# Which row groups first: the issue order of in_proj and gates ahead of ssm_out in a scan kernel

## The chip, the cores and the metric

The kernel runs on one core of a Trainium2 chip. The metric is the device time of one execution in microseconds (us).

## The reference, cut to what matters

Input x is (4, 128, 96, 96) in fp32. It is group-normalised, laid out as four sequences (rows and columns, each forwards and backwards), and each sequence goes through the same chain:

```python
t = _grouped1x1(x, in_proj_w, in_proj_b, G)          # 128 -> 512 channels, 4 groups of 32
u, gate = (t[:, :HID], t[:, HID:])                   # HID = 256
u = jax.nn.silu(u)
u = lax.conv_general_dilated(u, dw_w, ...)           # depthwise, 5 taps
s = _conv1x1(u, ssm_in_w)                            # 256 -> 32 channels
...                                                  # a, bb, cc from u; prefix sums: hst
u = u + _conv1x1(cc * hst + ssm_d[None, :, None] * s, ssm_out_w)   # 32 -> 256: "ssm_out"
u = _grouped1x1(u * jax.nn.sigmoid(gate), mix_w, mix_b, G)
return _conv1x1(u, out_proj_w, out_proj_b)
```

The four results are fused by one more 1x1 convolution and added to x.

## The kernel before

The work is cut into 384 units of 384 positions. A unit has `s` = 0 or 1 (two of the four sequences run side by side); unit numbers alternate between the two, so I call the units with `s` = 0 even and those with `s` = 1 odd. The program is software-pipelined by hand: step `t` does in_proj for a unit 8 ahead, and gates, ssm_out and gating for the unit 12 behind. TensorE's order in a step is set by this code, not by a scheduler:

```python
def unit(t):
    ...
    rows(t + UB ..., bi ..., bk)           # pf (in_proj), pg (gates), pz (ssm_out)
    ...
    accumulate(units[bi - 1], bk)          # py: mix, out_proj and fuse in one matrix
    gating(units[bi])
    conv(un, 0, bk); ...                   # pc
    proj(t - 1, 0)  or  proj(t - 2, 1)     # pp
```

The change is in `rows`, which issues 16 matmuls of 32x32 (in_proj and gates; each on its own of the 16 tiles of 32x32: in the trace of before their first records start within 0.11 us and take 0.51 us each, so all 16 run side by side) and then 8 more of 32x32 (ssm_out):

```python
def mm(o, col, lhsT, rhs, start, stop):
    r = slice(32 * col, 32 * col + 32)
    nc.tensor.matmul(o[r, : rhs.shape[-1]], lhsT, rhs, start=start, stop=stop, ...)

def rows(i, bi, bk):
    ...
    for c in range(4):                     # column group c of the array
        if front:
            for j in range(2):             # pf: row groups 0 and 1
                r = slice(32 * j, 32 * j + 32)
                m, q = (c, g) if by_taps(s, j) else (g, c)
                mm(pf[j], c, wn[r, 32 * m : 32 * m + 32], x_in[s][r, q, :], True, True)
        if gate:
            q, off = gate_at(bu)
            for j in range(2):             # pg: row groups 2 and 3
                r = slice(64 + 32 * j, 96 + 32 * j)
                mm(pg[j], c, gwn[r, 32 * c : 32 * c + 32],
                   x_in[bu["s"]][r, q, off : off + N], True, True)
    if gate:
        pz = ps.tile([P, 2, 512], F32, tag="z", ...)
        for c in range(4):
            for j in range(2):             # pz: row groups s and 2 + s
                r = slice(64 * j + 32 * bu["s"], 64 * j + 32 * bu["s"] + 32)
                mm(pz[:, j, :], c, w_so[r, ...], z[r, bu["p"], :], True, True)
        gv = wk.tile([P, 2, N], F32, tag="gv", ...)
        for j in range(2):                 # ScalarE: gate, reads pg[0], then pg[1]
            nc.scalar.activation(gv[:, j, :], pg[j][:, :N], AF.Tanh, ...)
        nc.vector.tensor_add(pz[:, :, :N], pz[:, :, :N], bu["u"])
```

Ssm_out thus uses row groups 0 and 2 in even units, 1 and 3 in odd ones.

## Time and profile before

| before | value |
|---|---|
| time, 3 runs | 2598.93 us median (2598.4 to 2602.78) |
| TensorE busy | 2548.0 us, 98% of the profiled execution |
| VectorE, ScalarE busy | 2025.2 us (78%), 1572.9 us (60%) |
| matmul records | 40016, two for each fp32 matmul |
| DMA | mean 52 GB/s |

A busy share near 100% on one engine says where to look, not that the engine computes all the time: the ends of matmuls in the profile are modelled, and TensorE counts as busy all through the stage below, in which tiles stand idle (pz 2's for some 180 ns, as an estimate: free near 683, used at 865). So the single records of a stage have to be read. Below, "the stage" is pf, pg and pz of one step, its zero is the first pf record, and its end is the start of py. Times in the stage are in ns and are medians over the stages of which all records are there (181 even and 182 odd ones).

### The profile page before, as it was taken

To read this page: it belongs to the slowest core of one execution; us is meant where nothing else is said; L and a number is where in the kernel's file an instruction comes from. 1 tells how busy PE (TensorE), PEld (TensorE's weight loads), DVE (VectorE), ACT (ScalarE), POOL (GpSimd) and SP (SyncE) were. 2 spreads that over 40 slices of the span, in tenths; PEclk is the share of its full clock that TensorE was granted. 3 is DMA by queue.
4 is the path that set the end of the run, shared out by engine and by line. 5 is a ranking of instruction groups with operands and counts; after the bars stand their busy time and mean duration, and the time that the engine had idled before them with its cause. 6 is when DMAs were issued, how large, how long until landed. Compare 5 with 4: busy or idle time off the path is not lost.

```text
span 2605.0 us, 89269 instructions
## 1 busy us (share of the span) xinstructions
PE 2548.0 (98%) x40016; PEld 966.1 (37%) x40016; DVE 2025.2 (78%) x2727; ACT 1572.9 (60%) x2912; POOL 506.4 (19%) x786
## 2 busy tenths in 40 slices
PE   6999999999999999999999999999999999999997
PEld 3333333333333333333333333333333333333331
DVE  3688878877878887777887887778876788778876
ACT  4666666666656666666665666666665666666652
POOL 4211121111111112111111112111111111111110
PEclk8999999999999999999999999999999999999998
DMA  5112111112331211111241111111132111111011
GB/s 141 46 45 51 47 34 30 35 29 85 94 97 45 51 41 28 35 30 36 84 134 54 50 45 37 30 36 29 45 117 76 36 30 36 33 32 36 23 41 56
DMA packets 79278, 134.18 MB, mean 52 GB/s; under 512 B 11440, under 2 KB 73392, under 8 KB 78896
## 3 DMA queue, kind: packets, MB, share of 16 engines
q1 hardware_dynamic: 76704, 127.64, 17.8%
q8 instruction: 315, 5.16, 0.8%
q10 hardware_dynamic: 2192, 0.83, 0.1%
q14 instruction: 67, 0.55, 0.1%
HBM read 109.55 MB, written 18.87 MB: 49 GB/s over the span
## 4 chain that ended last, share of the span: by engine, by line
PE 95%; DVE 1%; DMA 1%; ACT 1%; issue 0%; SPq 0%; DVEq 0%; ACTq 0%
PE pc L317 28%; PE py L317 21%; PE pp L317 20%; PE pz L317 12%; PE pf L317 11%; PE pg L317 2%; DMA out<-acc 1%; DVE t L480 0%; DVE gv L323 0%; ACT t L446 0%; ACT gv L373 0%; DMA acc<-in_xr 0%; DMA x_in<-in_xs 0%; ACT L446 0%; ACT L182 0%
## 5 line engine op out<-in xcount | busy, mean ns | idle before, releaser
L317 PE MATMUL pc<-sil,band 128*32 128x384 f32 x9216 | 820.4, 488 | 0.5 <-ACT gv L373 0.4
L403 ACT COPY u<-pc 128x384 f32<-128x384 f32 x576 | 275.8, 479 | 554.2 <-PE pc L317 553.0
L317 PE MATMUL pp<-u,w_proj 128*32 128x384 f32 x6144 | 594.7, 488 | 7.1 <-ACT std L182 5.6
L317 PE MATMUL py<-gv,w_fin 128*32 128x384 f32 x6144 | 586.8, 500 | 7.9 <-ACT gv L373 5.8
L418 DVE SCALAR_TENSOR_TENSOR pt<-sil,w_tap,pt 128x384 f32<-128x384 f32 x576 | 358.5, 622 | 180.5 <-ACT pt L416 164.5
L373 ACT ACTIVATE gv<-pg,bnorm 128x384 f32<-128x384 f32 x768 | 402.8, 576 | 106.6 <-PE pg L317 106.6
L317 PEld LDWEIGHTS pc<-sil,band 128*32 128x32 f32 x9216 | 297.0, 110 | 458.3 <-issue 363.8
L317 PE MATMUL pz<-t,w_so 32*32 32x384 f32 x6144 | 432.2, 494 | 6.6 <-DVE gv L323 6.4
L460 DVE TENSOR_TENSOR t<-pp,t 64x384 f32<-64x384 f32 x192 | 173.2, 902 | 287.2 <-ACT t L452 287.1
L377 DVE TENSOR_TENSOR pz<-pz,u 128x768 f32<-128x768 f32 x384 | 369.8, 963 | 16.5 <-PE pz L317 10.6
L317 PE MATMUL pf<-x_in,wn 32*32 32x385 f32 x6144 | 360.3, 504 | 10.4 <-DVE acc L505 9.4
L323 DVE SCALAR_TENSOR_TENSOR gv<-gv,pz 128x768 f32<-128x768 f32 x384 | 362.7, 944 | 0.1
L317 PE MATMUL pg<-x_in,wn 32*32 32x384 f32 x6144 | 360.3, 496 | 0.0
L449 POOL TENSOR_SCALAR t<-t 64x384 f32<-64x384 f32 x192 | 181.6, 946 | 879.2 <-ACT t L446 879.2
L317 PEld LDWEIGHTS pp<-u,w_proj 128*32 128x32 f32 x6144 | 224.6, 109 | 303.0 <-issue 258.1
L488 POOL COPY t<-t 64x384 f32<-64x384 f32 x192 | 95.9, 500 | 1154.5 <-DVE t L487 1154.5
L381 ACT ACTIVATE sil<-pf,bsilu 128x385 f32<-128x385 f32 x576 | 313.9, 585 | 4.3 <-PE pf L317 4.1
L317 PEld LDWEIGHTS py<-gv,w_fin 128*32 128x32 f32 x6144 | 161.9, 110 | 406.2 <-issue 275.2
L452 ACT ACTIVATE t<-pp,b_proj 64x384 f32<-64x384 f32 x192 | 110.6, 576 | 243.0 <-PE pp L317 122.6
L446 ACT ACTIVATE t<-pp,b_proj 128x384 f32<-128x384 f32 x192 | 208.6, 1086 | 70.6 <-PE pp L317 53.9
L317 PEld LDWEIGHTS pz<-t,w_so 32*32 32x32 f32 x6144 | 167.7, 103 | 166.3 <-issue 92.7
L450 POOL TENSOR_SCALAR t<-t 64x384 f32<-64x384 f32 x192 | 182.6, 951 | 15.9
(65 smaller groups left out, 1468.6 us busy)
## 6 DMA issues: line engine op xcount, KB each, us to landing
x_in<-in_xs SPq DMA_DIRECT2D x96, 385.0 KB, 4.3
x_in<-in_xs SPq DMA_DIRECT2D x384, 96.2 KB, 2.4
out<-acc SPq DMA_DIRECT2D x24, 768.0 KB, 5.1
xs<-in_xr SPq DMA_DIRECT2D x72, 192.0 KB, 2.3
acc<-in_xr SPq DMA_DIRECT2D x18, 768.0 KB, 4.6
acc<-in_xr SPq DMA_DIRECT2D x24, 192.0 KB, 3.8
w_fuse<-in_fuse_wT ACTq DMA_DIRECT2D x1, 256.0 KB, 4.1
w_proj<-in_proj_wT ACTq DMA_DIRECT2D x1, 128.0 KB, 4.8
```

The costliest lines, as they stand in the source:

```text
L317: nc.tensor.matmul(o[r, : rhs.shape[-1]], lhsT, rhs, start=start, stop=stop, skip_group_check=True)
L323: nc.vector.scalar_tensor_tensor(gv, gv, 1.0, bu["pz"][:, :, :N], ALU.add, ALU.mult)
L373: nc.scalar.activation(gv[:, j, :], pg[j][:, :N], AF.Tanh, bias=gbn[:, 2 + j : 3 + j], scale=0.5)
L377: nc.vector.tensor_add(pz[:, :, :N], pz[:, :, :N], bu["u"])
L381: nc.scalar.activation(sil[:, j, g, :], pf[j][:, : N + 1], AF.Silu, bias=bn[:, j : j + 1] if by_taps(s, j) else bsil[:, j, g : g + 1],)
L403: nc.scalar.copy(un["u"][:, j, :], pc[:, :N])
L418: nc.vector.scalar_tensor_tensor(un["u"][:, j, :] if k == K - 1 else part, src, w_tap[:, k : k + 1], part, ALU.mult, ALU.add,)
L446: nc.scalar.activation(ta[:, p, :], pp[:, :N], AF.Tanh, bias=b_proj[:, 0:1])
L449: nc.gpsimd.tensor_scalar(a, a, half, DMIN + half, ALU.mult, ALU.add)
L450: nc.gpsimd.tensor_scalar(a, a, 0.9999, 0.0001, ALU.min, ALU.max)
L452: nc.scalar.activation(tb[0:64, p, :], pp[0:64, :N], AF.Tanh, bias=b_proj[0:64, 1:2])
L460: nc.vector.tensor_mul(ta[0:64, p, :], pp[64:P, :N], ta[0:64, p, :])
```

## The change

The intent: pz should find its tiles free sooner. The matmuls on the two row groups that this unit's ssm_out uses come first, in the order in which pz will use the tiles; then the other two row groups. Nothing is added or removed.

```diff
-        for c in range(4):
-            if front:
-                for j in range(2):
-                    r = slice(32 * j, 32 * j + 32)
-                    m, q = (c, g) if by_taps(s, j) else (g, c)
-                    mm(pf[j], c, wn[r, 32 * m : 32 * m + 32], x_in[s][r, q, :], True, True)
-            if gate:
-                q, off = gate_at(bu)
-                for j in range(2):
-                    r = slice(64 + 32 * j, 96 + 32 * j)
-                    mm(pg[j], c, gwn[r, 32 * c : 32 * c + 32],
-                       x_in[bu["s"]][r, q, off : off + N], True, True)
+        so = bu["s"] if gate else 0
+        for e in (so, 1 - so):
+            r, rg = slice(32 * e, 32 * e + 32), slice(64 + 32 * e, 96 + 32 * e)
+            for c in range(4):
+                if front:
+                    m, q = (c, g) if by_taps(s, e) else (g, c)
+                    mm(pf[e], c, wn[r, 32 * m : 32 * m + 32], x_in[s][r, q, :], True, True)
+                if gate:
+                    q, off = gate_at(bu)
+                    mm(pg[e], c, gwn[rg, 32 * c : 32 * c + 32],
+                       x_in[bu["s"]][rg, q, off : off + N], True, True)
```

## The prediction

> **What bounds the kernel now.** I read the page first: busy shares, the slices, then the chain that ended last.
>
> ```profile
> PE 2548.0 (98%) x40016; PEld 966.1 (37%) x40016; DVE 2025.2 (78%) x2727; ACT 1572.9 (60%) x2912; POOL 506.4 (19%) x786
> PE 95%; DVE 1%; DMA 1%; ACT 1%; issue 0%; SPq 0%; DVEq 0%; ACTq 0%
> PE pc L317 28%; PE py L317 21%; PE pp L317 20%; PE pz L317 12%; PE pf L317 11%; PE pg L317 2%; DMA out<-acc 1%; DVE t L480 0%; DVE gv L323 0%; ACT t L446 0%; ACT gv L373 0%; DMA acc<-in_xr 0%; DMA x_in<-in_xs 0%; ACT L446 0%; ACT L182 0%
> ```
>
> TensorE carries 95% of the chain; VectorE at 78% and ScalarE at 60% follow it. So the change can only pay through TensorE's own stream. It touches pf (in_proj), pg (gates) and, through what runs after them, pz (ssm_out). I therefore read one unit in the timeline of PE and of PEld (weight loads) in the middle of the run.
>
> ```profile
> 1203.70 0.51 PE L317 MATMUL pf<-x_in,wn 32*32 32x385 f32 x2
> 1203.71 0.51 PE L317 MATMUL pg<-x_in,wn 32*32 32x384 f32 x2
> ...
> 1203.79 0.52 PE L317 MATMUL pg<-x_in,wn 32*32 32x384 f32 x2
> 1204.04 0.49 PE L317 MATMUL pf<-x_in,wn 32*32 32x385 f32 x2
> ...
> 1204.37 1.12 PE L317 MATMUL pz<-t,w_so 32*32 32x384 f32 x16
> 1205.43 0.85 PE L317 MATMUL py<-gv,w_fin 128*32 128x384 f32 x8
> ```
>
> Each fp32 matmul leaves two records. The 16 matmuls of pf and pg fill the 16 tiles of 32x32: 16 first records start in 0.11 us, and the 16 second ones begin 0.35 us after the first of all. Then pz, 8 matmuls on 8 of these tiles, takes 1.06 us to the start of py. Two rounds like those before would be near 0.7 us. So there is something to win in pz; the question is what withholds it. The weight loads tell:
>
> ```profile
> 1204.05 0.10 PEld L317 LDWEIGHTS pz<-t,w_so 32*32 32x32 f32 x1
> 1204.37 0.10 PEld L317 LDWEIGHTS pz<-t,w_so 32*32 32x32 f32 x1 [0.22 <-issue]
> 1204.56 0.20 PEld L317 LDWEIGHTS pz<-t,w_so 32*32 32x32 f32 x12
> ```
>
> Only the first pz matmul starts early. The second has its weights loaded at 1204.56, 0.19 us later, although its tile came free near 1204.38. "Issue" says that no semaphore of another engine ended this gap.
>
> I then took the single records of the 361 rows stages whose records are all there, counted in ns from the first pf record. They differ by 1 ns or so, in two classes: even units (ssm_out on row groups 0 and 2) and odd ones (1 and 3).
>
> - second record of the first matmul: 347 in both
> - first pz record: 671 even, 678 odd; that is 324 after the second record of its own tile (347 and 354)
> - weight load of the second pz matmul: 861 in both
> - first records of pz 2 to 8: 865 to 965 in both, 16.7 apart; their second records: up to 1309 in both
> - start of py: 1734 even, 1720 odd
>
> [...] Before the stage, pp's last four matmul records start at -436 to -416 with a length of 486, and end at 50 to 70. [...] Observed: the 14th starts at 87, and in odd units the 15th and 16th at 102 and 118, 16 apart instead of 6.7. [...]
>
> [...] pz 1's weights load at 349, two ns after a matmul on its own row group began. [...] 15 later matmuls start before the second record of the first.
>
> [...] from the last pp record to the first pf record is 416 ns, where rounds of one mode follow at 323; so some 93 ns per change, twice a unit. The change leaves the number of mode changes alone.
>
> **The change part by part.** It removes and adds no instruction: still 16 matmuls of pf and pg, 8 of pz, the same waits, the same banks. The program order of the built kernels shows pf and pg of the unit's own row groups alternating over the four columns, then the other two; pz in its old order. Waits for the second pair of banks move from place 2 and 4 to 9 and 10; in before none of them held the stage, since 416 is the start in every class.
>
> 1. First pz matmul. Its tile is now the first issued in both classes, so it starts at 671 in odd units too: 7 ns earlier. But its second record (993 to 1000) has slack: the stage ends with pz 8's second record at 1309. Worth 0.
> 2. Pz 2 to 8. Their tiles were free well before use already: pz 2's near 683 against 865, and pz 8's near 770 to 786 against 965. Freeing them earlier (pz 8's tile would be the 8th, free at about 347 + 47 + 323 = 717) buys nothing[...] Worth 0.
> 3. A small term. In odd units the first matmul now lies on row group 1, not 0. Py starts 14 ns sooner after row groups 1 and 3 than after 0 and 2, at equal ends of pz, so I take a matmul one row group further on to be finished about 14 ns sooner. If that holds, pz 2 to 8 and the stage end come 14 ns sooner in odd units: 192 x 14 ns = 2.7 us. I count half: 1.3 us.
> 4. Other engines. ScalarE gets one pf and one pg bank some 60 ns earlier, the others at the same time; it isn't on the chain.
> 5. First 8 units (no gates) and last 20 (gates only): orders change inside 16 or 8 matmuls on free tiles; 0.
>
> Sum: 2598.9 - 1.3, so about 2597.5 us.
>
> **The rivals.** (a) The full gain that the edit aims for. If pz followed tile by tile as they came free, pz 8 would start near 770 and end its second record near 1093 + 323 instead of 1309 + 323: 216 ns x 384 units = 83 us, 3.2%, so 2516. For it: the tiles of pz do stand idle. Against: in before pz 2's tile stands idle for 180 ns in every unit, so the order of tiles isn't the wait. (b) [...] pz 2's load would wait for the last matmul on its row group. That one starts its second record at about 441 to 447 (even) or 463 (odd) and would at 347 + 47 = 394 after the change: 50 to 70 ns x 384 = 19 to 27 us, so about 2575. Against: 861 is the same in both classes though these starts differ by some 20 ns. (c) Slower: two row groups instead of four share the first 8 matmuls, and if loads or moving data of one row group got in each other's way the 6.7 ns steps would widen. [...] Against: pz itself uses this order of tiles, and in the last units[...] the timeline shows it at full pace:
>
> ```profile
> 2590.72 0.21 PEld L317 LDWEIGHTS pz<-t,w_so 32*32 32x32 f32 x16 [1.56 <-issue]
> 2590.75 0.88 PE L317 MATMUL pz<-t,w_so 32*32 32x384 f32 x16 [0.89 <-DVE gv L323]
> 2591.56 0.53 PE L317 MATMUL py<-gv,w_fin 128*32 128x384 f32 x4
> ```
>
> Here the same 8 matmuls reach py in 0.81 us, not 1.06, with first records 6.7 ns apart. [...]
>
> **Range and chances.** The three runs of before spread from 2598.4 to 2602.8. With (b) given one chance in ten and (a) one in twenty, I take 2597.5, 8 in 10 between 2588 and 2603; faster by over 2% 0.05, within 2% 0.92, slower 0.03.
>
> **What would show it.** Right: first pz record at 671 in odd units; second pz load still at 861 (847 in odd ones if point 3 holds); pz to py near 1.06 us; the chain at 95% PE with the same shares. Wrong: the pz loads follow each other from about 0.68 us on, or at about 0.80 (rival b), or the 16 first records take more than 0.11 us (rival c).

## More of the kernel before

One more part matters in the end: five PSUM banks go round between the steps, by this table.

```python
banks.append({"f": (w, x), "g": (y, z), "y": y, "c": (z, None), "t": h})   # even step
banks.append({"f": (w, x), "g": (z, y), "y": h, "c": (z, y), "t": None})   # odd step
```

## The result, and the profile after

The changed kernel took 2591.26 us (median of 4 runs, 2590.04 to 2596.08), the kernel before, in the same rounds, 2598.66 us (4 runs, 2596.43 to 2602.78). The ratio is 0.9973, with a 95% interval of 0.9955 to 0.9991: within 2%, though the interval leaves out 1. Here and below a ratio is the mean time of one kernel's runs over that of the other's of the same rounds, so it is not quite the ratio of the medians quoted.

This is inside the predicted range, but 6 us below the predicted time. The page of the changed kernel, its busy shares and its chain of waits:

```profile
PE 2534.8 (98%) x40016; PEld 964.0 (37%) x40016; DVE 2023.1 (78%) x2727; ACT 1554.8 (60%) x2912; POOL 512.2 (20%) x786
...
PE 95%; DVE 1%; ACT 1%; DMA 1%; issue 0%; DVEq 0%; ACTq 0%
PE pc L317 29%; PE py L317 21%; PE pp L317 20%; PE pz L317 12%; PE pf L317 11%; PE pg L317 2%; DVE gv L323 0%; DVE t L479 0%; DMA out<-acc 0%; ACT t L445 0%; DMA acc<-in_xr 0%; ACT gv L372 0%; DMA x_in<-in_xs 0%; ACT L445 0%; ACT L182 0%
```

Nothing has moved but small shares: `pz` still has 12% of the chain. One difference is easily overlooked: `DMA out<-acc` went from 1% to 0%. It comes back below.

The timeline of one even unit, TensorE, after (columns: start in us, length in us, engine, line, operation, output and inputs, how many):

```profile
1228.30 0.51 PE L317 MATMUL pf<-x_in,wn 32*32 32x385 f32 x1
1228.31 0.51 PE L317 MATMUL pg<-x_in,wn 32*32 32x384 f32 x1
...
1228.41 0.50 PE L317 MATMUL pg<-x_in,wn 32*32 32x384 f32 x1
1228.65 0.48 PE L317 MATMUL pf<-x_in,wn 32*32 32x385 f32 x1
...
1228.97 1.12 PE L317 MATMUL pz<-t,w_so 32*32 32x384 f32 x16
```

And its weight loads (in brackets the idle time before a load, and what ended it):

```profile
1228.65 0.10 PEld L317 LDWEIGHTS pz<-t,w_so 32*32 32x32 f32 x1
1228.97 0.10 PEld L317 LDWEIGHTS pz<-t,w_so 32*32 32x32 f32 x1 [0.22 <-issue]
1229.16 0.18 PEld L317 LDWEIGHTS pz<-t,w_so 32*32 32x32 f32 x10
1230.02 0.16 PEld L317 LDWEIGHTS py<-gv,w_fin 128*32 128x32 f32 x8 [0.62 <-ACT gv L372]
```

Pf and pg now alternate one by one, as the edit wants. The second pz matmul still gets its weights 0.86 us into the stage (1229.16 - 1228.30), as before: the edit's aim is missed. But py starts 1.05 us after the first pz record (1230.02 - 1228.97), where it was 1.06. Over all stages:

| ns from the stage's start | first pz record | load of pz 2 | tanh of pg[0] | start of py |
|---|---|---|---|---|
| before, even | 671 | 861 | 1100 to 1680 | 1734 |
| before, odd | 678 | 861 | 1100 to 1682 | 1720 |
| after, even | 671 | 860 | 983 to 1565 | **1720** |
| after, odd | 671 | 860 | 1117 to 1700 | 1720 |

(In a quarter of the odd stages the tanh starts only near 2367. Py starts at 1720 in these too.)

So it is the even units that gained 14 ns, not the odd ones, and the column that moved with them is ScalarE's. ScalarE in this even unit, before (the stage starts at 1203.70):

```profile
1204.80 0.58 ACT L373 ACTIVATE gv<-pg,bnorm 128x384 f32<-128x384 f32 x1
```

and after (the stage starts at 1228.30):

```profile
1229.28 0.58 ACT L372 ACTIVATE gv<-pg,bnorm 128x384 f32<-128x384 f32 x1
```

The tanh that reads pg[0] began 1.10 us into the stage and now begins 0.98 us into it. Now the table of banks tells the rest: in an even step py ("y": y) is written to the very bank that pg[0] ("g": (y, z)) has just held. So the program has py wait for that tanh (the view of waits below names it 189 times). Before, the tanh ended at 1680 and py started 54 later, at 1734. In an odd step py goes to bank h, which neither gate of that step holds, and py starts at 1720, which is 411 after the last pz record (1309), about the 416 from pp to pf at the other change of tile shape; within one shape (pp) the records of a tile follow at 323. After, the tanh of even units ends at 1565, 155 before 1720, and holds nothing.

The view of TensorE's waits had said so before the change (columns: us in total, times, longest in us):

```profile
PEld py L317 <- ACT gv L373: 128.7, 189, 2.5
```

and says almost the same after it:

```profile
PEld py L317 <- ACT gv L372: 124.5, 190, 2.5
```

There are 192 even units, and all 189 waits lie in even units: all of them but three. I had seen this line and put it down to the 411 ns after pz, which odd units have too. It was both: of a mean gap of 0.68 us (128.7 over 189) only the last 14 ns were ScalarE's own, the rest is the wait for pz. The new line shows why the name alone proves nothing: ScalarE is still named, though it is now done 155 ns ahead.

Fourteen ns in 192 units are 2.7 us (the expectations below say 2.6). The measured difference is larger. In all runs together, before has a mean of 2598.1 us (25 runs) and after one of 2590.2 (10 runs): 7.9 us. So a second cause of some 5 us is to be found. I cut both traces at the starts of py. Units 140 to 188, with nothing but the steady stage, took 309.93 us before and 309.60 after: 0.33 us over 24 even units, 13.7 ns for each, which is the 14 ns above and nothing more. Units 280 to 296 took 111.4 us before and 105.6 after. There the third batch of four ends: its last rows of `acc` go out, the next batch's rows are loaded into the same place, and VectorE's first addition to it has to wait. The waits there, before:

```profile
DVE acc L505 <- DMA x_in<-in_xs: 8.2, 1, 8.2
...
PEld pf L317 <- DVE acc L505: 5.5, 1, 5.5
```

and after:

```profile
DVE acc L504 <- DMA x_in<-in_xs: 4.9, 1, 4.9
...
PEld pf L317 <- DVE acc L504: 2.2, 1, 2.2
```

TensorE's next pf waits for VectorE, VectorE for a transfer, and both waits became 3.3 us shorter. The transfer named is a load of x_in, but the one that counts is the last load of `acc`: in both traces the addition begins 0.32 us after that load has landed (2007.98 and 2008.30 us before, 2003.06 and 2003.38 after), and in a later run, even_only, it begins 0.07 us before the named load of x_in lands. The loads of `acc` wait in turn for transfers that go out. The first of the two pairs, as SyncE issues it, before:

```profile
1989.65 0.35 SPq L515 DMA_DIRECT2D out<-acc  x1
1994.63 0.33 SPq L517 DMA_DIRECT2D acc<-in_xr  x1
```

and after:

```profile
1988.02 0.35 SPq L514 DMA_DIRECT2D out<-acc  x1
1991.57 0.33 SPq L516 DMA_DIRECT2D acc<-in_xr  x1
```

The load is issued 0.02 us after the outgoing transfer has landed, which took 4.97 us before and 3.53 after. (The page's median over all 24 outgoing transfers went from 5.1 to 3.6; here it is this one that is waited for.) There is one more difference: by the trace's record of the granted clock, TensorE ran at half speed for 6.8 us of units 280 to 296 before, and for none of them after. So the 5.8 us there are 3.3 of a shorter wait and, as an estimate, up to 3.4 (half of 6.8) of clock.

After this, the questions for the experiments were: is it the place in TensorE's stream that holds pz (rather than tiles or row groups)? Do the even units win through ScalarE? And do the other 5 us belong to the change, to one half of it, or to chance?

### The profile page after: what moved, and what is told of

Its sections match the earlier page's. It is cut to its first block, busy times and chain, and to the rows that moved or that the text cites. A ratio compares the mean times of both kernels' runs of the same rounds, so it can differ in the third digit from the quotient of the medians.

```text
span 2589.8 us, 89224 instructions
## 1 busy us (share of the span) xinstructions
PE 2534.8 (98%) x40016; PEld 964.0 (37%) x40016; DVE 2023.1 (78%) x2727; ACT 1554.8 (60%) x2912; POOL 512.2 (20%) x786
## 4 chain that ended last, share of the span: by engine, by line
PE 95%; DVE 1%; ACT 1%; DMA 1%; issue 0%; DVEq 0%; ACTq 0%
PE pc L317 29%; PE py L317 21%; PE pp L317 20%; PE pz L317 12%; PE pf L317 11%; PE pg L317 2%; DVE gv L323 0%; DVE t L479 0%; DMA out<-acc 0%; ACT t L445 0%; DMA acc<-in_xr 0%; ACT gv L372 0%; DMA x_in<-in_xs 0%; ACT L445 0%; ACT L182 0%
## 5 line engine op out<-in xcount | busy, mean ns | idle before, releaser
L317 PE MATMUL py<-gv,w_fin 128*32 128x384 f32 x6144 | 580.0, 495 | 6.2 <-ACT gv L372 4.2
L445 ACT ACTIVATE t<-pp,b_proj 128x384 f32<-128x384 f32 x192 | 187.0, 974 | 70.2 <-PE pp L317 53.8
```

The costliest lines, as they stand in the source:

```text
L445: nc.scalar.activation(ta[:, p, :], pp[:, :N], AF.Tanh, bias=b_proj[:, 0:1])
```

## The experiments

All kernels are edits of `rows`. They use two helpers that hold the bodies of the loops of the changed kernel, unaltered: `pf_mm(e, c)` and `pg_mm(e, c)` issue one matmul of in_proj or gates on row-group pair `e` and column `c`; `pz_all()` issues the 8 of ssm_out. Every result was correct.

### The kernels again

The unchanged pair first. `after_again` is the changed kernel, in 5 rounds.

> The changed kernel once more, beside the runs of the others. Steady state as in its first profile: py starts 1720 ns after the first pf record in even and odd units, the second pz load comes at 860. If the steady 14 ns in every second unit are all that the order gives, the time lies 2 to 3 us below before (0.999); if the whole 7 us of the first comparison belong to the order, 0.997.

Measured: 2588.57 us (6 runs, 2584.11 to 2595.68) against 2597.84 for before (11 runs, 2588.83 to 2603.26), ratio 0.9968 [0.995, 0.9986]. The gain is there again, and larger than the 2.7 us of the steady stage. Units 140 to 188 again took 309.60 us, and units 280 to 296 took 104.8.

`before_again` and `before_third` are the kernel before with no edit, one look each, to see what two traces of one program differ in.

> The kernel before once more, for its profile. The steady parts must repeat (py at 1734 and 1720). If what the changed kernel gains beyond the steady 2.6 us is chance (waits for transfers and half-clock windows at the changes of batch and at the end), then the stretches in which the first profile of before was slow differ here: units 30 to 50 (136.4 us there, 134.65 in the changed kernel), 280 to 296 (111.4 against 105), 362 to 382 (111.7 against 104.3). If they belong to the order, they repeat within 0.5 us.

> The same as before_again, a third profile of before: chance gives values that differ among the three profiles, the order gives the same three times.

Measured: 2602.8 and 2601.14 us, where the timed runs of before in that call had a median of 2595.19 (3 runs). The steady stretch is the same to 0.01 us (309.92 in both). Others are not: units 30 to 50 took 136.4, 134.75 and 136.4 us in the three traces of before, the last 20 units 111.7, 111.6 and 109.4, and units 280 to 296 took 111.4, 108.9 and 111.5. In after, the two traces have 134.65 and 134.67, 104.34 and 104.35, 105.6 and 104.8. Such steps of 1.7 us and more come and go in one and the same kernel. By the rule set down above that speaks for chance in all three stretches, so a difference in one counts only if several traces bear it out.

### Only one half of the units

`even_only` and `odd_only` use the new order in the units of one kind, the old one in the others (`so == 1` in place of `so == 0` for odd_only):

```diff
-        for e in (so, 1 - so):
-            for c in range(4):
-                pf_mm(e, c)
-                pg_mm(e, c)
+        if gate and so == 0:
+            for e in (so, 1 - so):
+                for c in range(4):
+                    pf_mm(e, c)
+                    pg_mm(e, c)
+        else:
+            for c in range(4):
+                for e in range(2):
+                    pf_mm(e, c)
+                for e in range(2):
+                    pg_mm(e, c)
```

> New order only in units whose ssm_out uses row groups 0 and 2 (even), old order in odd units and in the front-only start. Theory A (in even units py writes the bank that held pg0, so it waits for ScalarE's tanh of pg0; the new order finishes pg0 sooner[...]): py at 1720 in even and in odd units, the whole steady gain of 2.6 us is here, 2591 to 2597 us. Rival B (a matmul on a later row group is finished sooner, my point 3 of the prediction, gain in odd units): py stays at 1734 in even units, no gain.

> New order only in odd units. Theory A: py 1734 even, 1720 odd, as before the change; time equal to before within 0.1%. Rival B: second pz load near 847 in odd units and py near 1706 there, 2.7 us less.

Measured: even_only 2596.69 us (6 runs, 2594.06 to 2603.27), ratio 1.000 [0.9983, 1.0017]; odd_only 2590.11 (6 runs, 2586.67 to 2598.28), ratio 0.9979 [0.9959, 0.9999]. The stages did as the ScalarE reading has it: with even_only, py of even units starts at 1720 (tanh 985 to 1565); with odd_only it stays at 1734 (tanh 1101 to 1682), though pz 1 moves from 678 to 671 in odd units. The steady stretch is 309.60 and 309.93. So the whole steady gain lies in the even units. The total went the other way: the half with the steady gain shows none in its interval's middle, and the half without it shows 5 us. The two intervals overlap, so the times alone do not tell the halves apart. My expectation for odd_only, equal to before, was right for the stage and missed the total. It looks as if the second cause goes with the odd units' order.

One more look at each half:

> The kernel with the new order only in even units once more, for its profile. Its first run had the slow values in units 30 to 50 (136.1 us) and 280 to 296 (111.3) and the fast one at the end (104.5). Chance: they change; order: they repeat.

> The kernel with the new order only in odd units, once more for its profile. Its steady part must repeat (1734 and 1720). If the output transfers go with the order of the odd units, their median to landing is again 3.5 to 3.6 us and units 280 to 296 take 104 to 108 us; if that was chance, they may be at 4.1 us or more and 109 us or more as in before.

Measured: even_again 2600.31 us, odd_again 2594.69, one look each. Steady stretch 309.60 and 309.91; units 280 to 296 took 111.1 and 105.1 us, where the first traces had 111.3 and 107.3: odd_only moved by 2.2 us and stayed below the values of before. The last 20 units do not repeat: 104.5 and then 110.0 us for even_only, 107.0 and 111.6 for odd_only.

### The order turned round

`reversed` takes the row groups that ssm_out does not use first:

```diff
-        for e in (so, 1 - so):
+        for e in (1 - so, so):
```

> The two row groups that ssm_out does not use are issued first, its own two last: the opposite of the change. Theory A: pg0 is the last bank finished in even units, so ScalarE's tanh of it starts near 1117 instead of 1100 and py near 1751 (17 ns later than before); in odd units pz 1 starts near 724 instead of 678, but the second pz load stays at 860 and py at 1720. Sum +3.3 us, about 2602. Rival C (tile order matters for pz): py later by about 50 ns in every unit, +19 us.

Measured: 2593.79 us (6 runs, 2589.68 to 2597.31), ratio 0.9984 [0.9966, 1.0002]. Now pg[0] comes last in even units. ScalarE in an even unit that starts at 1003.22:

```profile
1004.34 0.58 ACT L383 ACTIVATE gv<-pg,bnorm 128x384 f32<-128x384 f32 x1
```

and the weight loads of the same unit:

```profile
1004.97 0.16 PEld L317 LDWEIGHTS py<-gv,w_fin 128*32 128x32 f32 x8 [0.66 <-ACT gv L383]
```

The tanh ends at 1698 and py starts at 1750, 52 later, as it was 54 later before. This is the wait again, made longer by another order. In odd units py stays at 1720 although pz 1 has moved to 725, 54 later than after: the first pz record does have slack, and the order of tiles buys nothing. The load of pz 2 is still at 861. The steady stretch is 310.33 us, 0.40 more than before (24 even units by 17 ns), as worked out ahead. The total, expected above before, came out below it, so that expectation missed. Units 280 to 296 took 107.8 us, less than in before; whether that is the whole reason is not shown.

### Where in the stream the held matmul stands

In before and after, pz 2 is the 18th matmul of the stage, and its weights load at 861 and 860. If the place in the stream is what is held, another matmul put there must come at that time too. `pz_mid` puts the 8 of pz at places 9 to 16, ahead of the second half of pf and pg:

```diff
         for e in (so, 1 - so):
             for c in range(4):
                 pf_mm(e, c)
                 pg_mm(e, c)
-        pz_all()
+            if e == so:
+                pz_all()
```

> Program order: pf and pg of ssm_out's own row groups (8 matmuls), then pz (8), then pf and pg of the other two row groups (8). [...] the 17th matmul can start, the 18th and later are let in from about 860 ns on. So all 8 pz start their first records from 671 to about 720, and 7 of the 8 other matmuls start from 865 to 965, though their tiles are free from the start; py stays near 1720, time within 0.3% of the changed kernel. Rival (what holds pz back belongs to pz: its row groups, its operand or its banks): the other 8 matmuls start at about 50 to 110 on their free tiles, and pz stays late; or, if nothing holds it, py comes near 1500 and the time falls by up to 3%.

`pz_12` puts pz at places 13 to 20:

```diff
-        for e in (so, 1 - so):
-            for c in range(4):
-                pf_mm(e, c)
-                pg_mm(e, c)
-        pz_all()
+        for c in range(4):
+            pf_mm(so, c)
+            pg_mm(so, c)
+        for c in range(4):
+            pg_mm(1 - so, c)
+        pz_all()
+        for c in range(4):
+            pf_mm(1 - so, c)
```

> Program order: 12 of the 16 pf and pg matmuls (own row groups, then pg of the other), then pz, then the last 4 pf. [...] the 17th matmul is now the fifth pz, so pz 1 to 5 start at 671 to 710 and pz 6 is the first to be let in late, at about 860; then pz 7, 8 and the 4 pf follow 17 ns apart. py near 1720. Rival: the gap stays between pz 1 and pz 2, or is gone.

Measured: pz_mid 2590.41 us (4 runs, 2588.47 to 2599.4), ratio 0.9978 [0.9958, 0.9998]; pz_12 2590.6 (4 runs, 2589.3 to 2593.35), ratio 0.9975 [0.9959, 0.9992]. TensorE in a unit of pz_mid that starts at 993.74:

```profile
994.13 0.48 PE L317 MATMUL pg<-x_in,wn 32*32 32x384 f32 x1
994.27 0.48 PE L317 MATMUL pf<-x_in,wn 32*32 32x385 f32 x1
994.41 0.53 PE L317 MATMUL pz<-t,w_so 32*32 32x384 f32 x8
994.59 0.48 PE L317 MATMUL pf<-x_in,wn 32*32 32x385 f32 x1
994.60 0.50 PE L317 MATMUL pg<-x_in,wn 32*32 32x384 f32 x1
```

Now all 8 first pz records start together (994.41; 671 to 719 over all stages), and it is pf and pg of the other two row groups that are held, on eight tiles which stand idle from the start of the stage. The 17th matmul starts alone at 994.27 (533), and its second record follows at 856, 27 after the modelled end of the first matmul's second record (829). The 18th starts at 994.60 (864), on a row group that no earlier matmul of the stage has used. The first records of places 18 to 24, at 864 to 964, come before the second records of pz, places 9 to 16, at 993 to 1040. Weight loads in a unit of pz_12 that starts at 996.91:

```profile
997.26 0.13 PEld L317 LDWEIGHTS pz<-t,w_so 32*32 32x32 f32 x5
997.58 0.13 PEld L317 LDWEIGHTS pz<-t,w_so 32*32 32x32 f32 x5 [0.19 <-issue]
997.77 0.10 PEld L317 LDWEIGHTS pz<-t,w_so 32*32 32x32 f32 x1
```

Five pz loads (places 13 to 17) follow each other in a run, first at 997.26 and for the second pass at 997.58, and the sixth (place 18) comes at 997.77, 0.86 us into the stage. In these two kernels the operand, the tile and the row group at place 18 are others than before, and the time is the same. So it is the place in the stream that is held: sixteen matmuls and one more start, the next one at 860. What holds it was not shown. The number of matmuls matters: the last 20 units have no in_proj and so 16 matmuls of this shape in the stage, not 24, and there no pz is held. In four of the first five odd ones in the trace of before, the first records of pz start at 53 to 445, the last second record at about 1040, and py at 1449 in place of 1720. Why the new place of pz is no gain is in the same numbers: with 24 matmuls in the stage, the last one's second record starts near 1309 in every order up to here, and py near 1720 (1734 and 1750 where it waits for ScalarE). Units 140 to 188 took 309.60 and 309.65 us, and neither kernel beats the changed one (mean of all runs 2590.2 us).

### Fewer matmuls in the stage

`pgz_wide` asks what fewer matmuls in the stage are worth: pf as 8 matmuls of 32x32, but each half of pg and of pz as one matmul of 32x128 (12 in place of 24).

```diff
+                nc.tensor.matmul(pg[e][:, :N], gwn[rg, :],
+                                 x_in[bu["s"]][rg, q, off : off + N], start=True, stop=True, ...)
...
+                for j in range(2):
+                    r = slice(64 * j + 32 * bu["s"], 64 * j + 32 * bu["s"] + 32)
+                    nc.tensor.matmul(pz[:, j, :N], w_so[r, 128 * j : 128 * j + 128],
+                                     z[r, bu["p"], :], start=True, stop=True, ...)
...
         for e in (so, 1 - so):
             for c in range(4):
                 pf_mm(e, c)
-                pg_mm(e, c)
-        pz_all()
+        pg_wide(so)
+        pg_wide(1 - so)
+        pz_all()
```

(The last line's `pz_all` is the one with the two wide matmuls.)

> [...] the four column matmuls of pg share their moving data, and so do those of pz, so each four become one with 128 output rows. The rows stage then has 8 pf, 2 pg and 2 pz matmuls[...]. If tiles of 32x32 and of 32x128 run side by side, py starts near 1410 instead of 1720 ns: 384 x 0.31 = 119 us less, about 2475. [...] py starts near 2220: 384 x 0.5 = 190 us more, about 2785.

Measured: 2814.32 us (2 runs, 2813.55 to 2815.09), ratio 1.0828 [1.076, 1.0896]: slower, near the 2785 expected if the wide matmuls do not overlap pf. TensorE in a unit that starts at 872.33:

```profile
872.33 0.88 PE L317 MATMUL pf<-x_in,wn 32*32 32x385 f32 x16
873.13 0.59 PE L377 MATMUL pg<-x_in,wn 32*128 32x384 f32 x2
...
873.56 0.49 PE L377 MATMUL pg<-x_in,wn 32*128 32x384 f32 x2
873.57 1.11 PE L370 MATMUL pz<-t,w_so 32*128 32x384 f32 x3
```

The first wide pg starts at 806, which is 412 after the last pf record (394): a round of 323 and some 89 more, where the tile shape changes. Its second record follows 427 later (at 1233), where it is 347 for the first pf of before. Then two more pz rounds follow, at 1557 and 1879; the first of them is 324 after that second record, and the second pz matmul is on a row group that a gate uses too. That this is its reason was not tested apart. Py starts at 2385 in even units and at 2288 in odd ones. Here fewer matmuls did not pay: with their shape came the gap of 412 and the two late rounds of pz. So this run does not test the number of matmuls by itself.

### The first gate at the very front

`pg0_first` issues pg[0] before everything else in even units, and leaves odd units in the old order. It asks two things: what is left when ScalarE's wait is taken away by other means, and whether the second cause goes with the odd units' order.

```diff
+        if gate and so == 0:
+            for c in range(4):
+                pg_mm(0, c)
+            for c in range(4):
+                pf_mm(0, c)
+                pf_mm(1, c)
+                pg_mm(1, c)
+        else:
+            ...                            # the old order, as in even_only
```

> Only in even units, and not in ssm_out's order: the four columns of pg0 first, then pf0, pf1, pg1 column by column as before. Theory A (py waits for ScalarE to have read pg0's bank): pg0 ends earlier still, its tanh starts near 985 or earlier, py at 1720 in even units, though pz 1's tile is now the 5th issued (its first record near 700). If instead the order of the tiles that pz uses made the 14 ns, py stays at 1734. The odd units keep the old order, so by what the other profiles show the output transfers should be slow here (median 4.1 us or more to landing).

Measured: 2606.75 us in one look, before 2599.66. Times in this stage count from the first pg record, which here comes first. The tanh now runs from 916 to 1497 in even units and does not hold py. Py, expected at 1720, starts at 1744, but now because pz itself is late: the first records of pz 2 to 8 come at 863, 880, 896, then 939 to 989, with one gap of 43 in place of 17, and the last second record at 1333 in place of 1309. From there to py it is 411 (1744 - 1333), as in odd units before (1720 - 1309 = 411), where even units of before have 425. So the 14 ns of ScalarE are gone, and some 25 ns of another kind have come in. One difference goes with the late fifth pz matmul: here the fourth matmul of the stage carries the semaphore update that releases ScalarE, and in every other order of 24 matmuls the first seven carry none. Whether that is the reason was not shown.

The orders together show what the start of the tanh goes with. It starts at 916, 984, 1051, 1100 and 1117 when the last matmul of pg[0] stands at place 4 (pg0_first), 8 (after, even units), 12 (pz_12, odd), 15 (before) and 16 (after, odd): 16.7 ns for a place, the pace at which pz 2 to 8 start. The matmul's second record itself moves only from 440 to 394 between places 15 and 8.

Its trace has 111.2 us in units 280 to 296, like the other kernels with the odd units' old order. But its outgoing transfers landed in a median of 3.6 us, like those of the kernels with the new one, so the expectation of 4.1 or more missed. The next section shows why the median misleads.

### The stage changes, all traces together

| us, one value for each trace | odd units in the old order: before (3), even_only (2), pg0_first | new or reversed order: after (2), odd_only (2), reversed, pz_mid, pz_12 |
|---|---|---|
| units 280 to 296 | 111.4, 108.9, 111.5; 111.3, 111.1; 111.2 | 105.6, 104.8; 107.3, 105.1; 107.8; 106.7; 105.2 |
| transfer that goes out before unit 288, to landing | 5.0, 4.6, 5.1; 5.5, 5.1; 4.9 | 3.5, 3.4; 3.9, 3.4; 3.3; 3.6; 3.4 |
| wait of the first addition to `acc` | 8.2, 6.5, 8.2; 8.3, 7.7; 8.2 | 4.9, 4.2; 4.9, 4.3; 5.1; 4.7; 4.4 |
| clock at half speed in units 280 to 296 | 6.8, 3.4, 6.8; 6.8, 6.8; 6.8 | 0, 0; 3.4, 0; 3.4; 3.4; 0 |

Six traces of six on one side, seven of seven on the other, at least 1.1 us apart. The stretch was picked from the first pair of traces; the later ones bear it out. So in this stretch the difference goes with the order in odd units, and its path can be followed: one outgoing transfer lands 0.7 us or more sooner, the load behind it and the addition follow, and the clock is at half speed for less time. Pg0_first has the long stretch with a median of 3.6 us over its 24 outgoing transfers, but the one that counts took 4.9. What stays open is why this transfer lands later with the old order.

Two things speak against making this a rule. At the other two changes of batch the traces do not sort by the order: units 84 to 104 took 134.6, 133.2 and 131.6 us in before and 136.4 and 136.3 in after, units 186 to 206 took 133.4, 135.9 and 134.4, and 133.9 and 134.7. And the largest difference between the traces of before and after lies elsewhere, in the last 20 units: 111.7, 111.6 and 109.4 against 104.3 and 104.3, with the clock at half speed for 20.5, 20.5 and 13.7 us against 6.8 and 6.8. Even_only and odd_only each had values 4.6 us or more apart there in their two traces, so I give that part to no order.

## Why the prediction was right or wrong

**The bound: right, and now shown.** Parts 1 and 2 of the sum gave the new order of tiles no worth, because the second pz matmul's weights load at 861 in both classes, with its tile free since about 683. Measured: 860 after, and with other orders the 18th matmul at about 860 whatever it was (pz_mid, pz_12). So the place in the stream is shown; what holds it is not. One observation was weaker than the prediction has it: the 14th matmul at 87 is not late (13 steps of 6.7), only the 16th is (109 in even units, 118 in odd ones), and in odd units the 15th (102). The first pz record in odd units moved to 671 as predicted, and moving it to 725 (reversed) cost odd units nothing, so its slack is shown too.

**The rivals: all refuted.** (a) The full gain, pz tile by tile: the tiles come free and stand idle. (Its 83 us were sized with the old time of the last tile, near 770 (764 in even units, 787 in odd ones). With the 717 of part 2 it is 269 ns, or 103 us.) (b) The wait for the last matmul on the row group: the pz load would be at about 0.80 us and is at 0.86, and in pz_mid the 18th matmul starts only at 864 on a row group that is idle. (The starts that it compares are 440 in even units, not 441 to 447, and 463 in odd ones.) (c) Slower steps: the first records still take 0.11 us.

**Point 3, the small term: wrong.** The step read "so I take a matmul one row group further on to be finished about 14 ns sooner", and gave 1.3 us to odd units. Odd units kept 860 and 1720. The 14 ns between even and odd units were real, but their cause was not the row group: in even units py waits for the tanh of pg[0], whose bank it takes over. The change brings pg[0] from place 15 of 16 to place 8 in even units, so the tanh ends 115 ns sooner and the even units gain 14 ns, the whole difference. The number I used was right and I gave it to the wrong half of the units: 2.7 us in place of 1.3. That the sign of the sum was right is luck.

**Point 4: wrong by the same 14 ns.** "ScalarE ... isn't on the chain" followed from its busy share and from the chain's 0%. Its pg[0] bank came not "some 60 ns earlier" but 117 (1100 to 983), by the 16.7 ns for a place. And 2.7 us of 2599 are 0.1%, which the page prints as 0%. At that size a rounded share cannot rule anything out; the bank table and the view of waits could have.

**Part 5: nearly right.** In the last 20 units, given 0, py of those odd units came at 1422 in place of 1449: 27 ns in a few units.

**What the sum had no term for.** The rest of the 7.9 us, some 5. I had looked for effects in the steady stage alone, and had given the stretches where the batch changes no worth. In units 280 to 296 the traces of after are 5.4 us shorter than those of before, and 13 traces show that this goes with the odd units' order; why is open. That 2.7 and 5.4 come near the 7.9 between the means does not close the account: the traces of before and after lie 13.1 us apart, with 6.6 in the last 20 units and 3.2 the other way at the first change of batch. Odd_only alone has 5.5 by its ratio (0.9979 of 2598 us), reversed 4.2 although its steady stage is 3.3 longer, and even_only should show 2.7, which its interval allows.

The range of 2588 to 2603 held, because the spread of before had been put into it, not because these terms were known.

## What to carry to other kernels

Before reordering matmuls so that tiles come free sooner, look whether the next matmul starts late on a tile that is already idle. Here pz 2 did (its weights at 861, its tile free near 683), its place in the instruction stream was what counted (860 to 865 for the 18th matmul in before, after, reversed, pz_mid and pz_12), and another order of tiles gained nothing. In the last 20 units the stage was shorter with fewer matmuls of the same tile shape (py at 1449 with 16 of them, at 1720 with 24); with a wider shape it was not (2288 and 2385). When two classes of one stage differ by a few ns, look at which buffer each takes over and from whom, before blaming the geometry. And compare traces stretch by stretch with several traces of the same program beside them, since a kernel's own stretches differ by more than such a change is worth (the last 20 units of even_only by 5.5 us between two traces, where the steady gain is 2.7); look at the granted clock of each stretch, and at the one transfer that is waited for, not at the median of its kind.
